# Seven block products for four in the first layer of a mixture-of-experts FFN, with the sums of weights made and kept in the first FFN

## The chip, the cores and the metric

The kernel runs on one core of a Trainium2 chip. The core has a matrix engine (TensorE, in the profile PE, with its weight loads as PEld), a vector engine (VectorE, DVE), an activation engine (ScalarE, ACT), a general engine (GpSimd, POOL) and a queue engine that issues transfers (SyncE, SP). They run side by side and wait for each other by semaphores. The metric is the time of one execution on the device in microseconds (us), the median of several runs.

## The reference

The model is an FFN, an attention-like memory layer and the same FFN again, on 8192 rows of 256 values:

```python
x = L0_attn_hidden
x = x + 0.5 * _L0_ffn_ref(_layernorm(x), gate_w, w1, w2)
x = x + _L0_attn_ref(_layernorm(x), ...)
x = x + 0.5 * _L0_ffn_ref(_layernorm(x), gate_w, w1, w2)
```

Both FFNs use the same weights. An FFN sends every row to the best of E = 8 experts, each with room for CAP = 320 rows:

```python
expert_input = jnp.einsum('tec,td->ecd', sec_mask, tokens)
h = jax.nn.relu(jnp.einsum('ecd,edf->ecf', expert_input, w1))
expert_output = jnp.einsum('ecf,efd->ecd', h, w2)
out = jnp.einsum('tec,ecd->td', combine_weights, expert_output)
```

So the first layer of an expert is a product of 320x256 with 256x1024, and the second layer one of 320x1024 with 1024x256, all in float32.

## The kernel before

`macaron` (from L1309 on) runs the first router, the first FFN (`experts(..., "f1")`), the memory layer (`attention`) and the second FFN (`experts(..., "f2", idle=4)`) one after the other. The router of the second FFN is computed inside the attention.

`experts` goes through the experts e = 0 to 7. Inside it, the instructions of PE, DVE, ACT and POOL stand in the order in which the Python code issues them; each engine works through its own queue in that order. Transfers issued by SP are placed by the compiler. For one expert:

- `gather(e)` (L287) fetches the expert's rows `xg` by three indirect DMAs of POOL, `gate_of(e)` (L298) their gate values by three more. `xg` has four buffers.
- `center` (L311 to L313) takes the mean off each row, on DVE: `bn_stats`, `bn_aggr` and a subtraction for each of three groups of 128 rows (the last has 64). `turn` (L323, L327) transposes the rows on PE into PSUM tiles `pt`, and ACT copies them to `xT`, two chunks of 128 features by 320 rows.
- The first layer, `hidden` (L388, L395): for each of FC = 8 blocks f of 128 hidden values, two matmuls with a 128x128 block of `w1t` as the stationary operand and the 320 columns of `xT` as the moving one, accumulated in a PSUM tile `ph`; ACT applies Relu and writes `hT`. For expert 0 this is done in two passes, over the first 128 rows and then over the other 192, because its rows arrive late.
- The second layer: first the last 64 rows (L419, `py`, both halves of the output in different column groups), then twice 128 rows (L443), with `hT` as the stationary operand. DVE multiplies by the gate and adds the row itself (L429 `xh`, L450 `xo`), and POOL scatters the result by indirect DMAs (L432, L453).

PSUM has eight banks of 512 columns. Before, the tiles of tag `t` (transposes) have three of them, tag `h` (`ph`) three and tag `y` (`py`, and others) two.

Where the rows of an expert lie is found by `Slots`. `begin(q)` counts for the pair of experts 2q and 2q+1: two matmuls into `d_ps`, a copy to `dg` by ACT, one matmul into `b_ps` (L209), a comparison `began` on DVE (L212). `counts(q)` (L228) makes two PSUM tiles `r_ps`, one for each expert of the pair, and `tokens(e)` (L246 to L254) turns one of them into row indices by six short DVE instructions. These searches are put between the blocks of the first layers of experts 0, 1 and 2, by the table `searches`. `keep` issues matmuls whose results nobody reads.

`Weights.load(e)` issues the DMAs of `w1[e]` and `w2[e]`, 1 MB each, from SP; two buffers each. The DMAs for expert e+1 are issued at the start of expert e.

## Time and profile before

| | us |
|---|---|
| median of three runs | 813.77 |
| lowest and highest run | 808.3 and 816.86 |
| the profiled execution | 822.0 |
| its span, from the first instruction to the last | 820.2 |

In the profiled execution the first FFN's experts run from about 51 to 217 us, the attention follows, and the second FFN's experts run from 654 to 820. The granted clock of TensorE was 0.951 of full speed on average. A profile of this kind names a group of instructions by its line in the kernel, its engine, its operation and its tiles (output <- inputs) and gives busy time, mean duration of one and what ended the idle time before. Durations of matmuls overlap, since they are pipelined, so that what one costs is read from start to start.

### The profile page before, as it was taken

The page shows a single profiled execution, that of the slowest core. Times are in us where ns is not written, and L with a number is a line of the kernel's source. Part 1 is how long each engine was busy: PE and PEld are TensorE (multiplying, and loading weights), DVE is VectorE, ACT ScalarE, POOL GpSimd, SP SyncE. Part 2 cuts the span into 40 slices and gives each one's busy share as a digit, 9 for nine tenths or more (in the row PEclk, how much of TensorE's full clock was granted, in tenths as well). Part 3 has the DMA queues.
Part 4 walks back from the last instruction along what each step waited for, and adds up shares of the span by engine and source line. Part 5 has one row for each costly group of instructions (what it writes and reads, how often), then busy time and mean ns, then how long its engine had stood idle before and what let it go on. Part 6 is the DMA issues. An engine that isn't in the chain of part 4 may idle for free. (4 is left out here: it accounts for less than half of the span.)

```text
span 820.2 us, 13993 instructions
## 1 busy us (share of the span) xinstructions
PE 746.9 (91%) x5368; PEld 549.3 (67%) x5368; DVE 452.2 (55%) x941; ACT 348.3 (42%) x756; POOL 472.2 (58%) x606
## 2 busy tenths in 40 slices
PE   7988899999658999899999989999878789999997
PEld 5666678777525485766668576776765466788775
DVE  7772242220228978889886878868743623422220
ACT  5421122222047576757665766756432222122221
POOL 6555244441134778888887889876854344444411
PEclk9998899999968999999997999889988999999999
DMA  9994444451224243443543442434415723454420
GB/s 298 370 382 149 136 138 140 146 166 43 73 66 86 80 104 95 117 152 79 181 105 129 136 121 83 88 119 106 129 60 187 256 72 106 136 175 138 145 68 22
DMA packets 110946, 110.41 MB, mean 135 GB/s; under 512 B 12384, under 2 KB 103904, under 8 KB 110880
## 3 DMA queue, kind: packets, MB, share of 16 engines
q1 hardware_dynamic: 73152, 66.43, 27.2%
q10 hardware_dynamic: 31840, 31.53, 12.2%
q0 software_dynamic: 5888, 11.57, 4.2%
q8 instruction: 42, 0.69, 0.3%
q14 instruction: 24, 0.20, 0.1%
HBM read 78.80 MB, written 30.64 MB: 133 GB/s over the span
## 5 line engine op out<-in xcount | busy, mean ns | idle before, releaser
L395 ACT ACTIVATE hT<-ph 128x320 f32<-128x320 f32 (+2 forms) x144 | 58.4, 408 | 228.8 <-PE ph L388 202.5
L388 PE MATMUL ph<-xT,w1t 128*128 128x320 f32 (+2 forms) x576 | 146.9, 410 | 1.5 <-ACT xT L336 1.5
L388 PEld LDWEIGHTS ph<-xT,w1t 128*128 128x128 f32 x576 | 103.5, 192 | 36.9 <-ACT xT L336 2.3
L443 PE MATMUL py<-w2t,hT 128*128 128x256 f32 x512 | 121.6, 394 | 5.8 <-issue 4.3
L443 PEld LDWEIGHTS py<-w2t,hT 128*128 128x128 f32 x512 | 98.7, 196 | 25.0 <-issue 9.2
L429 DVE SCALAR_TENSOR_TENSOR xh<-py,gate,xg 64x128 f32<-64x128 f32 x32 | 11.2, 350 | 125.2 <-PE py L419 104.2
L450 DVE SCALAR_TENSOR_TENSOR xo<-py,gate,xg 128x256 f32<-128x256 f32 x32 | 15.5, 484 | 93.3 <-PE py L443 93.3
L1144 PE MATMUL pre<-wg,xT 128*128 128x256 f32 x256 | 62.0, 403 | 2.7 <-DVE m L903 2.7
L808 PE MATMUL pre<-xT,w 128*64 128x512 f32 x256 | 61.4, 603 | 0.8 <-ACT kk L840 0.8
L1144 PEld LDWEIGHTS pre<-wg,xT 128*128 128x128 f32 x256 | 51.1, 203 | 11.7 <-DVE m L903 3.3
L298 POOL DMA_INDIRECT gate<-gate_d,get x48 | 45.3, 943 | 21.4 <-issue 13.1
L1188 POOL TENSOR_TENSOR xo<-xo,xr 128x512 f32<-128x512 f32 x32 | 42.9, 1353 | 19.8 <-DVE xo L1182 17.5
L710 ACT ACTIVATE xt<-xt,ln_nm,lx_t 128x256 f32<-128x256 f32 x64 | 34.4, 592 | 24.2 <-POOL ln_nm L705 24.2
L1182 DVE SCALAR_TENSOR_TENSOR xo<-tail,rs,gate 128x256 f32<-128x256 f32 x64 | 27.1, 476 | 26.2 <-DMA out<-xo 12.6
L997 DVE TENSOR_TENSOR gc<-ehd,c 128x1536 f32<-128x1536 f32 x16 | 40.0, 2540 | 0.3
L453 POOL DMA_INDIRECT out<-xo,put x16 | 15.8, 989 | 40.1 <-DVE xo L450 26.7
L453 POOL DMA_INDIRECT x<-xo,put x16 | 15.8, 988 | 38.9 <-DVE xo L450 34.6
L808 PEld LDWEIGHTS pre<-xT,w 128*64 128x64 f32 x256 | 15.8, 136 | 30.3 <-issue 22.3
L432 POOL DMA_INDIRECT x<-xh,put x8 | 8.1, 1006 | 47.7 <-DVE xh L429 47.7
L909 POOL TENSOR_TENSOR abq<-qq,ab 128x512 f32<-128x512 f32 x16 | 33.6, 2105 | 0.9 <-DMA ab<-kept 0.9
L717 PE MATMUL pre<-ident,xt 128*128 128x128 f32 x128 | 21.1, 299 | 14.3 <-ACT xt L710 12.9
L287 POOL DMA_INDIRECT xg<-x,get x24 | 23.4, 974 | 17.6 <-issue 6.1
(259 smaller groups left out, 1622.4 us busy)
## 6 DMA issues: line engine op xcount, KB each, us to landing
w1t<-w_in SPq DMA_DIRECT2D x16, 1024.0 KB
w2t<-w_in SPq DMA_DIRECT2D x16, 1024.0 KB
xt<-hidden_in SPq DMA_DIRECT2D x16, 512.0 KB
x<-xt SPq DMA_DIRECT2D x16, 512.0 KB
xt<-x ACTq DMA_DIRECT2D x16, 512.0 KB
xr<-x ACTq DMA_DIRECT2D x16, 512.0 KB
x<-xo ACTq DMA_DIRECT2D x14, 512.0 KB
out<-xo ACTq DMA_DIRECT2D x14, 512.0 KB
```

The source lines that it names most:

```text
L298: nc.gpsimd.indirect_dma_start(out=gate[:, s : s + 1], out_offset=None, in_=slots.gate, in_offset=bass.IndirectOffsetOnAxis(ap=slots.get[: ...
L388: nc.tensor.matmul(ph[:, at_slots], lhsT=a[:, c, f * P : (f + 1) * P], rhs=at[:, c, at_slots], start=(c == 0), stop=(c == 1),)
L395: nc.scalar.activation(hT[:, f, at_slots], ph[:, at_slots], AF.Relu)
L443: nc.tensor.matmul(py[:, :H], lhsT=hT[:, f, s * P : (s + 1) * P], rhs=b[:, f, :], start=(f == 0), stop=(f == FC - 1),)
L453: nc.gpsimd.indirect_dma_start(out=dst, out_offset=bass.IndirectOffsetOnAxis(ap=slots.put[:, e, s : s + 1], axis=0), in_=xo[:, s, :], in_o ...
L710: self.nc.scalar.activation(x, x, AF.Identity, bias=u.nm[:, j : j + 1], scale=u.r16[:, j : j + 1])
L808: self.nc.tensor.matmul(ps[self.half[r], :], lhsT=self.w3[:, k, f * D : (f + 1) * D], rhs=u.xT[:, k].rearrange("h (p r t) -> h p r t", p=N ...
L909: self.nc.gpsimd.tensor_tensor(u.abq[:, n], u.kv[2], u.ab[:, n], ALU.mult)
L997: self.nc.vector.tensor_tensor(u.gc[:, layer], g.unsqueeze(2).to_broadcast([P, B, 3, D]), u.c3.rearrange("s n j -> s j n").unsqueeze(3).to ...
L1144: self.nc.tensor.matmul(ps[:, q * H : (q + 1) * H], lhsT=u.xT[:, k, j * P : (j + 1) * P], rhs=self.wg[:, k, :], start=(k == 0), stop=(k == 1),
L1182: self.nc.vector.scalar_tensor_tensor(u.xo[h][:, j, :], self.out_of(u, h, j), u.rs[h][:, j : j + 1], u.gate[n][:, j % 2, :], ALU.mult, ALU ...
L1188: self.nc.gpsimd.tensor_tensor(u.xo[h][:, two], u.xo[h][:, two], u.xr[h][:, two], ALU.add)
```

## The change

Both the row halves of `xT` (2 x 160 columns), the two chunks of features and each pair of f blocks are taken as a 2x2 block problem. The plain way has eight block products of 160 columns, done as four matmuls of 320. The changed second FFN does seven block products of 160 columns for each of the four pairs g from expert 1 on (class `First`); expert 0 and the whole first FFN keep the plain way (`plain`). The seven products need four sums of blocks of w1 (`Weights.sums`, 128x512 each) and four sums of blocks of `xT` (`row_sums`, DVE). The results are combined in `hT` by ACT and DVE, in five steps `one` to `five`, of which `four` and `five` of a pair are issued within the next pair; Relu comes last, partly in place.

The sums of weights are made in the first FFN, by GpSimd, at the start of each expert from 1 on, into the four buffers that held the router's rows (tag `xt`), and stored to DRAM (`keep`, 1 MB an expert). The second FFN loads them (1 MB more an expert, two buffers).

With it go these edits: the PSUM banks become two each of tags `x`, `z` (the first layer), `t` (transposes and searches) and `y`; `center` subtracts on ACT, with the sign turned (mean minus row), so that every Relu has a scale of -1; `center(e+2)` is issued after `xh` of expert e, `center(1)` inside expert 0; `gather(e+3)` is issued after the scatter of `xh`, `gate_of(e+1)` at the start of expert e; `begin` is split into `begin` and `began_at`; the searches for later pairs move from the first layers of experts 1 and 2 to the second layers of experts 1, 2 and 3; the part of the second layer on 64 rows takes block f = 6 last; two instructions instead of three prepare `wg` in the attention.

```diff
--- before
+++ after
-    def begin(self, q, between=lambda n: None):
-        nc, sh, pool, pp = self.sh.nc, self.sh, self.pool, self.pp
-        d_ps = pp.tile([P, 512], F32, tag="y", name="d_ps", bufs=2)
+    def begin(self, q, tag="t"):
+        nc, sh = self.sh.nc, self.sh
+        d_ps = self.bank(tag, "d_ps")
         two = slice(q * P, (q + 1) * P)
         nc.tensor.matmul(d_ps[:, :P], lhsT=self.mask[:, two], rhs=sh.tri, start=True, stop=False)
         nc.tensor.matmul(d_ps[:, :P], lhsT=self.prev[:, two], rhs=sh.ntri, start=False, stop=True)
         dg = self.dg[:, q, :]
         nc.scalar.copy(dg[:, :P], d_ps[:, :P])
-        between(1)
-        b_ps = pp.tile([P, 512], F32, tag="h", name="b_ps")
-        nc.tensor.matmul(b_ps[:, 0:1], lhsT=sh.before, rhs=dg[:, P - 1 : P], start=True, stop=True)
-        between(1)
-        began = pool.tile([P, NS * P], F32, tag="began", name="began", bufs=2)
-        nc.vector.tensor_scalar(began, sh.jrow, b_ps[:, 0:1], None, ALU.is_ge)
-        self.began = began
-    def counts(self, q, tag="y"):
+        self.last = dg[:, P - 1 : P]
+    def began_at(self, tag="t"):
+        nc, sh = self.sh.nc, self.sh
+        b_ps = self.bank(tag, "b_ps")
+        nc.tensor.matmul(b_ps[:, 0:1], lhsT=sh.before, rhs=self.last, start=True, stop=True)
+        self.began = self.pool.tile([P, NS * P], F32, tag="began", name="began", bufs=2)
+        nc.vector.tensor_scalar(self.began, sh.jrow, b_ps[:, 0:1], None, ALU.is_ge)
+    def counts(self, q):
...
-            self.pp.tile([P, 512], F32, tag=tag, name="r_ps", bufs={"y": 2, "h": 3}[tag])[
-                :, : NS * (P + 1)
-            ].rearrange("p (s r) -> p s r", s=NS)
+            self.bank("t", "r_ps")[:, : NS * (P + 1)].rearrange("p (s r) -> p s r", s=NS)
...
+    def first(self, e):
         a = self.pool.tile([P, 2, F], F32, tag="w1", name="w1t")
         self.nc.sync.dma_start(a, self.w1[e].rearrange("(c p) f -> p c f", p=P))
-        b = self.pool.tile([P, FC, H], F32, tag="w2", name="w2t")
+        self.w[e] = a
+        v = a.rearrange("p c (g i m) -> p c g i m", i=2, m=P)
+        self.a[e] = [[v[:, c, :, i, :] for c in range(2)] for i in range(2)]
+    def second(self, e):
+        b = self.b[e] = self.pool.tile([P, FC, H], F32, tag="w2", name="w2t")
         self.nc.sync.dma_start(b, self.w2[e].rearrange("(c p) d -> p c d", p=P))
-        self.at[e] = a, b
-def experts(sh, routed, src, dst, weights, dr, name, idle=0):
+    def sums(self, e):
+        s = self.s[e] = self.place().rearrange("p a b -> p (a b)")[:, : 2 * F].rearrange(
+            "p (n g m) -> p n g m", n=4, m=P
+        )
+        if e in self.kept:
+            self.nc.sync.dma_start(s, self.kept[e])
+            return
+        (a11, a12), (a21, a22) = self.a[e]
+        for n, (x, y, op) in enumerate(
+            (
+                (a21, a22, ALU.add),
+                (s[:, 0], a11, ALU.subtract),
+                (a11, a21, ALU.subtract),
+                (a12, s[:, 1], ALU.subtract),
+            )
+        ):
+            self.nc.gpsimd.tensor_tensor(s[:, n], x, y, op)
+    def keep(self, e):
+        self.kept[e] = self.dr.tile([P, 4, FC // 2, P], F32, name=f"sums{e}")
+        self.nc.sync.dma_start(self.kept[e], self.s[e])
+def experts(sh, routed, src, dst, weights, dr, name, idle=0, seven=False):
...
-        pp = st.enter_context(tc.tile_pool(name=f"{name}_p", bufs=3, space=PSUM))
-        slots = Slots(sh, rp, pp, dr, routed)
+        pp = st.enter_context(tc.tile_pool(name=f"{name}_p", bufs=2, space=PSUM))
+        bank = lambda tag, name: pp.tile([P, 512], F32, tag=tag, name=name)
+        slots = Slots(sh, rp, bank, dr, routed)
...
-            ln = ep.tile([P, NS, 8], F32, tag="ln", name="ln")
             xn = ep.tile([P, NS, H], F32, tag="xn", name="xn")
             for s in range(NS):
-                nc.vector.bn_stats(ln[:, s, :6], xg[:, s, :])
-                nc.vector.bn_aggr(ln[:, s, 6:], ln[:, s, :6])
-                nc.vector.tensor_scalar(xn[:, s, :], xg[:, s, :], ln[:, s, 6:7], None, ALU.subtract)
+                ln = ep.tile([P, 8], F32, tag="ln", name="ln", bufs=4)
+                nc.vector.bn_stats(ln[:, :6], xg[:, s, :])
+                nc.vector.bn_aggr(ln[:, 6:], ln[:, :6])
+                nc.scalar.activation(xn[:, s, :], xg[:, s, :], AF.Identity, bias=ln[:, 6:7], scale=-1.0)
...
+        def turn(xn, xT):
+            pts = [bank("t", "pt") for _ in range(2)]
...
+        def row_sums(xT):
+            t = ep.tile([P, 4, HC], F32, tag="xs", name="xs", bufs=1)
+            v = xT.rearrange("p c (j n) -> p (c j) n", j=2)
+            nc.vector.tensor_tensor(t[:, 0:2], v[:, 1:4:2], v[:, 0:2], ALU.subtract)
+            nc.vector.tensor_tensor(t[:, 2], v[:, 3], t[:, 0], ALU.subtract)
+            nc.vector.tensor_tensor(t[:, 3], v[:, 2], t[:, 2], ALU.subtract)
+            return t
...
                 hidden(f, slice(P if e == 0 else 0, CAP))
-                for search, n in searches.get((e, f), ()):
-                    search(n)
                 if (e, f) == (0, 1):
+                    slots.counts(1)
+                    slots.tokens(2)
                     rows.append(gather(2))
-                    gates += [gate_of(1), gate_of(2)]
+                    gates.append(gate_of(1))
+                    xns[1] = center(rows[1])
+                if (e, f) == (0, 3):
+                    slots.tokens(3)
+                if (e, f) == (0, 5):
+                    slots.begin(2)
+                if (e, f) == (0, 6):
+                    slots.began_at()
+            return hT
...
+        class First:
+            def __init__(self, e, xT, t):
+                self.a, self.s = weights.a[e], weights.s[e]
+                self.b = xT.rearrange("p c (j n) -> p c j n", j=2)
+                self.t = t
+                self.hT = ep.tile([P, FC, CAP], F32, tag="hT", name="hT")
+                self.x, self.z, self.u, self.v = {}, {}, {}, {}
+            def product(self, out, a, g, b, start=True, stop=True):
+                nc.tensor.matmul(
+                    out, lhsT=a[:, g, :], rhs=b, start=start, stop=stop, skip_group_check=True
+                )
+            def one(self, g):
+                x = self.x[g] = bank("x", "x")
+                self.product(x[:, :HC], self.s[:, 1], g, self.t[:, 2])
+                self.product(x[:, HC : 2 * HC], self.a[0][0], g, self.b[:, 0, 0], stop=False)
+                p6 = ep.tile([P, HC], F32, tag="p6", name="p6")
+                nc.scalar.copy(p6, x[:, :HC])
+                u = self.u[g] = ep.tile([P, HC], F32, tag="u", name="u", bufs=3)
+                nc.vector.tensor_tensor(u, x[:, HC : 2 * HC], p6, ALU.add)
+            def two(self, g):
+                z = self.z[g] = bank("z", "z")
+                self.product(z[:, :HC], self.s[:, 2], g, self.t[:, 1])
+                self.product(z[:, HC : 2 * HC], self.a[1][1], g, self.t[:, 3])
+                self.product(z[:, 2 * HC : 3 * HC], self.s[:, 0], g, self.t[:, 0], stop=False)
+                v = self.v[g] = ep.tile([P, 1, HC], F32, tag="v", name="v")
+                nc.vector.tensor_tensor(v[:, 0], z[:, :HC], self.u[g], ALU.add)
+            def three(self, g):
+                nc.vector.tensor_tensor(
+                    self.hT[:, 2 * g + 1, :].rearrange("p (j n) -> p j n", j=2),
+                    self.z[g][:, HC : 3 * HC].rearrange("p (j n) -> p j n", j=2),
+                    self.v[g].to_broadcast([P, 2, HC]),
+                    ALU.add,
+                )
+            def four(self, g):
+                x = self.x[g]
+                self.product(x[:, HC : 2 * HC], self.a[0][1], g, self.b[:, 1, 0], start=False)
+                nc.scalar.activation(self.hT[:, 2 * g, :HC], x[:, HC : 2 * HC], AF.Relu, scale=-1.0)
+            def five(self, g):
+                z = self.z[g]
+                self.product(z[:, 2 * HC : 3 * HC], self.s[:, 3], g, self.b[:, 1, 1], start=False)
+                nc.vector.tensor_tensor(self.hT[:, 2 * g, HC:], z[:, 2 * HC : 3 * HC], self.u[g], ALU.add)
+            def relu(self, f, a=0):
+                h = self.hT[:, f, a:]
+                nc.scalar.activation(h, h, AF.Relu, scale=-1.0)
...
+        if seven:
+            weights.sums(1)
...
+        searches = {
+            (1, 0): lambda: slots.counts(2),
+            (1, 1): lambda: slots.tokens(4),
+            (1, 2): lambda: slots.tokens(5),
+            (2, 0): lambda: slots.begin(3),
+            (2, 2): slots.began_at,
+            (3, 0): lambda: slots.counts(3),
+            (3, 1): lambda: slots.tokens(6),
+            (3, 2): lambda: slots.tokens(7),
+        }
+        search = lambda *at: searches.get(at, lambda: None)()
+        for e in range(E):
+            xg, b = rows[e], weights.b[e]
+            if 0 < e < E - 1:
+                if seven:
+                    weights.sums(e + 1)
+                weights.first(e + 1)
+                weights.second(e + 1)
+            if e + 1 < E and e > 0:
+                gates.append(gate_of(e + 1))
+            if e > 0 and not seven:
+                weights.sums(e)
+                weights.keep(e)
+            if not seven or e == 0:
+                hT = plain(e, xn, xT)
+            else:
+                first = First(e, xT, t)
+                hT = first.hT
+                for g in range(G):
+                    first.one(g)
+                    if g > 0:
+                        first.four(g - 1)
+                    first.two(g)
+                    if g > 0:
+                        first.five(g - 1)
+                    first.three(g)
+                    if g > 0:
+                        first.relu(2 * g - 1)
+                        first.relu(2 * g - 2, HC)
+                first.four(G - 1)
+                first.relu(2 * G - 1)
             if e + 1 < E:
-                xT = turn(xn)
+                xT = ep.tile([P, 2, CAP], F32, tag="xT", name="xT")
+                turn(xn[e + 1], xT)
+            if seven and e > 0:
+                first.five(G - 1)
+                first.relu(2 * G - 2, HC)
+            if seven and e + 1 < E:
+                t = row_sums(xT)
             gate = gates[e]
...
+            order = [f for f in range(FC) if f != FC - 2] + [FC - 2]
+            for f in order:
...
+            search(e, 0)
...
+            if e + 2 < E:
+                xn[e + 2] = center(rows[e + 2])
+            search(e, 1)
...
+            if e + 3 < E:
+                rows.append(gather(e + 3))
...
+                if s == 0:
+                    search(e, 2)
...
+        for x, by, op in ((bg, 256.0, ALU.add), (ng, 1.0 / 16.0, ALU.mult)):
+            nc.vector.scalar_tensor_tensor(
+                self.wg, self.wg, by, x.to_broadcast([P, 2, H]), ALU.mult, op
+            )
...
+        place = lambda: rp.tile([P, NI // 4, H], F32, tag="xt", name="s", bufs=4)
...
+        experts(sh, sh.second, x2, out, weights, dr, "f2", idle=4, seven=True)
```

## The prediction

> **What bounds the kernel now.** The page comes first, for the shares of the engines.
>
> ```profile
> span 820.2 us, 13993 instructions
> ...
> PE 746.9 (91%) x5368; PEld 549.3 (67%) x5368; DVE 452.2 (55%) x941; ACT 348.3 (42%) x756; POOL 472.2 (58%) x606
> ```
>
> TensorE (PE) works for nine tenths of the span, but a share over the span says nothing of one stage. So next the table by stretches, for the second FFN (640 to 820 us).
>
> ```profile
> 720.00:740.00 20.00, 20.00 (x111) 16.03 (x110) 4.77 (x14) 4.35 (x10) 9.48 (x10) 1.00 0.45 142
> 740.00:760.00 20.00, 20.00 (x111) 15.98 (x111) 4.29 (x13) 4.35 (x10) 9.00 (x10) 1.00 0.44 148
> 760.00:780.00 20.00, 20.00 (x110) 15.69 (x109) 5.62 (x18) 4.68 (x11) 9.05 (x10) 1.00 0.47 145
> ```
>
> The columns are PE, PEld, DVE, ACT, POOL, the granted clock, the DMA share and GB/s. PE is never idle here, at clock 1.00; DVE is busy 28% at most, ACT 23%, DMA under half. In this stage a nanosecond off PE is a nanosecond off the end, as long as the others can follow. What one expert costs PE is read from the PE timeline: start, duration, group, number of records. A float32 matmul of the program stands as two records, so the 16 matmuls of a first layer are 32.
>
> ```profile
> 753.06 7.17 PE L443 MATMUL py<-w2t,hT 128*128 128x256 f32 x32
> 760.07 8.78 PE L388 MATMUL ph<-xT,w1t 128*128 128x320 f32 x32
> 768.69 0.86 PE L323 MATMUL pt<-ident,xn 128*128 128x128 f32 x6
> 769.48 1.97 PE L419 MATMUL py<-w2t,hT 128*64 128x128 f32 x32
> ```
>
> From start to start: first layer 768.69 - 760.07 = 8.62 us (269 ns a record), transposes 0.79, the 64-row part of the second layer about 1.9, the rest 7.01 (219 ns a record of 256 columns): 18.3 us an expert.
>
> **The seven products on PE.** Per pair of f blocks four matmuls of 320 columns (8 records) become seven of 160 (14 records). No record of 160 columns with its own weight load is in the trace, but expert 0 has its neighbours.
>
> ```profile
> 654.05 1.60 PE L388 MATMUL ph<-xT,w1t 128*128 128x128 f32 x12 [0.46 <-ACT xT L336]
> 655.49 0.38 PE L335 MATMUL pt<-ident,xn 128*128 128x128 f32 x2
> ...
> 661.49 2.87 PE L388 MATMUL ph<-xT,w1t 128*128 128x192 f32 x16
> 664.20 0.38 PE L203 MATMUL d_ps<-tri,mask_b 128*128 128x128 f32 x2
> ...
> 665.16 0.38 PE L209 MATMUL b_ps<-dg,before 128*128 128x1 f32 x2 [0.35 <-ACT dg L206]
> ...
> 666.79 0.86 PE L323 MATMUL pt<-ident,xn 128*128 128x128 f32 x6
> ```
>
> 128 columns: 1.44/12 = 120 ns. 192: 2.71/16 = 169 ns. With 219 at 256 and 269 at 320 these lie on one line, so 160 columns are halfway between the first two: 144.7 ns. One expert: 56 x 144.7 = 8.10 us for 8.62, a gain of 0.52, and 3.6 us over experts 1 to 7. Here a rule of the Trainium skill ("TensorE: Matmul & The Clock Gate", Back-to-back issue gap) would promise more: the warm gap is the columns over 2.4 GHz plus 2.5 ns. The 320-column record fits it with two passes (640/2.4 + 2.7), and 160 would then take 135.8 ns: 7.60 us an expert, 7.1 us in all. The same section warns that the isolated gap undercounts a narrow matmul with a weight load in front. The rows side with the warning: at 128 columns the rule gives 109, the trace 120. I take the rows; 7.1 is the far end of the gain, and 160 columns as dear per column as 128 (150 ns, gain 1.5 us) the near end.
>
> **Who must follow PE.** In before ACT does one Relu of 320 columns per f. Now each pair needs four instructions of ACT and four of DVE in its 14 x 144.7 = 2.03 us. Rows of like shape:
>
> ```profile
> L246 DVE TENSOR_TENSOR upto<-r_ps,jcol 128x384 f32<-128x384 f32 x14 | 7.7, 550 | 5.9 <-PE r_ps L228 5.9
> L246 DVE TENSOR_TENSOR upto<-r_ps,jcol 128x128 f32<-128x128 f32 x2 | 0.6, 290 | 2.4 <-PE r_ps L228 2.4
> ...
> L395 ACT ACTIVATE hT<-ph 128x320 f32<-128x320 f32 x112 | 48.8, 437 | 214.2 <-PE ph L388 190.2 <-issue 15.4 <-PE pt L323 4.5
> L395 ACT ACTIVATE hT<-ph 128x192 f32<-128x192 f32 x16 | 5.2, 330 | 9.6 <-PE ph L388 7.8 <-PE b_ps L209 1.2 <-issue 0.5
> ```
>
> DVE at 160 columns 0.32 us, at 320 0.48: 3 x 0.32 + 0.48 = 1.44. ACT: 3 x 0.31 + 0.44 = 1.4. Both fit into 2.03, with some 0.1 for gaps. The order of waits matters more. A z bank comes back when `five` of two pairs earlier has been added by DVE; followed through (PE result, p6 copy, u, v, five, three) that is about 0.3 us before `two` wants it. I charge nothing inside a stage. After the last pair `five` waits for `three` on DVE: the transposes between cover all but 0.1 us in experts 1 to 6; expert 7 has none, so about 0.9 there. Together 1.5 us. The row sums (three short DVE instructions) are due 7 us later and cost nothing; centering goes from DVE to ACT, which is idle in the second layer.
>
> **Expert 0, in both FFNs.** PSUM banks of tag t fall from three to two, and they now serve the counts, `begin`, `began_at` and the transposes; row statistics of expert 1 move into DVE's queue between `tokens(2)` and `tokens(3)`.
>
> ```profile
> 661.59 0.56 DVE L246 TENSOR_TENSOR upto<-r_ps,jcol 128x384 f32<-128x384 f32 x1 [4.91 <-PE r_ps L228]
> ...
> 663.52 0.55 DVE L246 TENSOR_TENSOR upto<-r_ps,jcol 128x384 f32<-128x384 f32 x1
> ...
> 665.58 0.42 DVE L212 TENSOR_SCALAR began<-jrow,b_ps 128x384 f32<-128x384 f32 x1
> ```
>
> Statistics and mean of three rows take 3 x 0.67 = 2.0 us (0.42 + 0.18 + gaps). `tokens(3)` then starts at 665.5 for 663.5, lets its bank go at 666.9, and `began` behind it ends at about 667.9. The second bank for the transposes is free only then: they start at 667.9 for 666.79, and the second layer queued behind them is late by the same. Its cover, DVE's idleness before the counts, is given up. 1.2 us, in two FFNs 2.4; if the compiler finds another free bank, 0. The first transposes also wait for ACT to center three rows instead of DVE: 0.1 each. The last `begin` and its b_ps leave expert 1's first layer for expert 2's second, where dg is long there, so the 0.35 wait of PE for it goes, twice: -0.7.
>
> **GpSimd in the first FFN.** Its stage holds nine indirect DMAs at 1.25 us from start to start, 11.3 of 18.3 us. Four sums of 128x512 come on top: near row `xo<-xo,xr`, 1353 ns, so 5.6 us with gaps; dear row `abq`, 2105 ns, so 8.6. The sum is 16.9 to 19.9 us: it just fits, or falls back 1.6 us a stage. Behind the sums wait the scatter of xh (ready at 12 us, sums done at 11 to 14) and the gather of expert e+3; this gather is used a stage later, and from expert 5 on there are none. I take 0; with that cover gone it would be up to 6 us. The stores of 1 MB (7 of them) queue on SP ahead of the next weights, which cannot start before their buffer is free at 8.6 us and are due 25 us later: 0. The same for 1 MB more loaded per expert in the second FFN: 8 us of DMA at some 370 GB/s in 18. The first weights already start at 638.5, and the extra load is queued after all of them. The two-for-three wg instructions stand in the idle start of the attention: 0.
>
> **Sum:** -3.6 + 1.5 + 2.4 + 0.2 - 0.7 = -0.2 us. The profiled execution took 822.0 us (820.2 and 1.8 around), 8.2 above the median of 813.77; its sum is 821.8, and I carry the difference over to the median: **813.6 us**. What tells a change of this kernel from none is about 1%, 8.1 us.
>
> **Rivals.** *An old stall goes (faster).* In the second layer of expert 0 PE stands still in this execution, in both FFNs.
>
> ```profile
> 673.39 0.94 POOL L298 DMA_INDIRECT gate<-gate_d,get  x1 [0.30 <-issue]
> ...
> 676.38 0.71 DVE L429 SCALAR_TENSOR_TENSOR xh<-py,gate,xg 64x128 f32<-64x128 f32 x2 [10.37 <-PE py L443]
> ```
>
> xh starts 2.05 us after the last of six gate gathers, though its product ended at 669.6; in the first FFN the gap is the same. PE lost 5.9 and 6.7 us there. Expert 0 now has three of these gathers, ending 3.75 us earlier. If the stall follows them, 7.5 us go, and with the b_ps wait in expert 1 (3.95 and 1.35 us in this execution) 4 to 5 more: about -12, **802 us**. Against it: experts 3 to 6 have the same gathers and no stall at all, and the timed runs lie below the profiled one, so part of this may not be in them.
>
> *The tight chain stalls PE (slower).* In expert 2 of the second FFN two Relus whose products ended at 712.83 and 713.90 came at 715.08 and 715.41, about 2 us late. Three ph banks hid that. With 0.3 us of slack such a delay stops PE, and DVE now waits for PE and ACT four times a pair. 2 us in each of seven stages is 14 us, **827 us**. It decides from 0.3 us per pair on, that is, when DVE's four instructions need over 2.3 us instead of 1.5; 28 pairs at 0.43 cost 12 us. Against it: the like rows above, and clean stages 3 to 6.
>
> *GpSimd binds the first FFN:* +6, 820 us. *The rule's price holds:* -3.5, 810 us. Both are inside 1%, as is my forecast.
>
> **Chances.** Forecast with these two 0.53; stall gone 0.19; tight chain 0.28. The forecast's own range is 808 to 820. To leave out no more than 2 in 10 I reach from 803 to 828.
>
> **What would show it.** Records of 160 columns 145 ns apart at full clock (136 would be the rule); first layers of 8.1 to 8.3 us in experts 1 to 7; transposes of expert 0 about 1 us later, waiting for DVE; no b_ps wait in expert 1; sums of 1.3 to 2.1 us on GpSimd, with no PE wait behind them. PE waiting for DVE v or five inside a stage would prove the slower rival; xh of expert 0 near 672 us the faster.

## The result and the profile after

The kernel after took 822.15 us (median; 817.48 to 829.45) beside 811.14 for the kernel before on the same chip: 1.0114 of it, 95% interval 1.0065 to 1.0163. It is slower; my forecast was no change at 813.6, with slower given 0.28. Of the experiments, half_sums, free_scatters, dve_best and before_again ran on a third chip and the other eight on a second. On both the kernel before takes 797 us; the kernel after takes 820.8 on the second, 1.0275 of it (1.0227 to 1.0323), and was not run on the third. How before differs from chip to chip is told with the run before_again.

The page of the kernel after, its span, the busy times and PE's and POOL's rows of slices (one slice is 20.4 us):

```profile
span 815.7 us, 14687 instructions
...
PE 731.2 (90%) x5536; PEld 555.9 (68%) x5536; DVE 483.7 (59%) x1025; ACT 378.7 (46%) x860; POOL 509.2 (62%) x634
...
PE   7978999999318989999998999999878979999996
...
POOL 6545666654521879888889888876873444444431
```

PE is busy 15.7 us less than in before. But in slices 11 and 12 it falls to 3 and 1: that is the passage from the first FFN to the attention. PE's timeline there, last the idle time before a row and what ended it, first in before and then in after:

```profile
217.40 1.56 PE L598 MATMUL pre<-w,ones 128*128 128x384 f32 x4 [0.58 <-DVE xo L450]
218.79 1.03 PE L598 MATMUL pre<-wg,ones 128*128 128x256 f32 x4
232.75 2.80 PE L717 MATMUL pre<-ident,xt 128*128 128x128 f32 x8 [12.93 <-ACT xt L710]
```

```profile
208.71 1.56 PE L759 MATMUL pre<-w,ones 128*128 128x384 f32 x4 [0.58 <-DVE xo L609]
210.11 1.03 PE L759 MATMUL pre<-wg,ones 128*128 128x256 f32 x4
241.62 2.81 PE L877 MATMUL pre<-ident,xt 128*128 128x128 f32 x8 [30.48 <-ACT xt L870]
```

PE is through with the first FFN 8.7 us earlier than in that profile of before, and begins the attention 8.9 us later: 30.48 us idle for 12.93. ACT is not the cause; it waits for rows of x1 that are not loaded yet. The load (`xt<-x`, issued from ACT's DMA queue) goes out 3.15 us after the last scatter of `xo` in before (at 217.62) and 3.12 after it in after (at 226.48), first before and then after:

```profile
220.77 1.51 ACTq L692 DMA_DIRECT2D xt<-x  x3
...
229.60 1.63 ACTq L852 DMA_DIRECT2D xt<-x  x3
```

The scatters are POOL's. Its timeline for the last expert, in after:

```profile
212.05 1.32 POOL L614 DMA_INDIRECT x<-xo,put  x1 [2.19 <-DVE wg L761]
213.38 1.28 POOL L293 TENSOR_TENSOR s<-w1t 128x512 f32<-128x512 f32 x1
214.74 1.26 POOL L293 TENSOR_TENSOR s<-s,w1t 128x512 f32<-128x512 f32 x1
215.96 1.26 POOL L293 TENSOR_TENSOR s<-w1t 128x512 f32<-128x512 f32 x1
217.18 1.26 POOL L293 TENSOR_TENSOR s<-w1t,s 128x512 f32<-128x512 f32 x1
218.59 0.99 POOL L588 DMA_INDIRECT x<-xh,put  x1 [0.15 <-issue]
223.32 0.97 POOL L614 DMA_INDIRECT x<-xo,put  x1 [3.73 <-DMA x<-xh,put]
226.48 0.97 POOL L614 DMA_INDIRECT x<-xo,put  x1 [2.19 <-issue]
```

PE ended the last `py` at 208.1, and DVE the last `xo` at 208.7. POOL scatters expert 6's `xo` at 212.05, only then makes the sums of expert 7, and scatters expert 7's three parts at 218.59, 223.32 and 226.48. It is a stage behind. The second thing to see is the idle time between two scatters: each waits for a semaphore until the one before has landed in x1 ("<-DMA x<-xh,put").

The second FFN did what the change is for. Some records from its last expert, PE's timeline:

```profile
793.71 0.43 PE L440 MATMUL x<-xs,s 128*128 128x160 f32 x2
...
795.61 0.43 PE L440 MATMUL x<-xs,s 128*128 128x160 f32 x2
...
799.41 0.43 PE L440 MATMUL x<-xT,w1t 128*128 128x160 f32 x2
800.39 0.54 PE L440 MATMUL z<-xT,s 128*128 128x160 f32 x2 [0.54 <-DVE hT L465]
```

From pair to pair 795.61 - 793.71 = 1.90 us for 14 records, 136 ns each, for 2.03 us and 144.7 in my sum.

So three theories stood. **A, GpSimd's backlog**: its stage in the first FFN is longer than PE's, and the attention waits for what is left over. **B, the stores**: 1 MB more an expert holds up the scatters' landings, whoever makes the sums. **C, the second FFN**: the loss lies in the tight chain there, and the passage would be made good elsewhere.

### The profile page after: what moved, and what is told of

It reads as the page before. It is cut to its first block, busy times and chain, and to the rows that moved or that the text cites. A ratio compares the mean times of both kernels' runs of the same rounds, so it can differ in the third digit from the quotient of the medians.

```text
span 815.7 us, 14687 instructions
## 1 busy us (share of the span) xinstructions
PE 731.2 (90%) x5536; PEld 555.9 (68%) x5536; DVE 483.7 (59%) x1025; ACT 378.7 (46%) x860; POOL 509.2 (62%) x634
## 5 line engine op out<-in xcount | busy, mean ns | idle before, releaser
L602 PE MATMUL py<-w2t,hT 128*128 128x256 f32 x512 | 115.3, 382 | 0.3 <-issue 0.3
L602 PEld LDWEIGHTS py<-w2t,hT 128*128 128x128 f32 x512 | 95.7, 190 | 16.3 <-issue 3.4
L394 PE MATMUL ph<-xT,w1t 128*128 128x320 f32 (+2 forms) x352 | 81.9, 387 | 4.4 <-ACT xn L352 2.5
L394 PEld LDWEIGHTS ph<-xT,w1t 128*128 128x128 f32 x352 | 60.2, 190 | 22.8 <-ACT xn L352 2.9
L401 ACT ACTIVATE hT<-ph 128x320 f32<-128x320 f32 (+2 forms) x88 | 33.4, 388 | 78.0 <-PE ph L394 61.2
L1304 PE MATMUL pre<-wg,xT 128*128 128x256 f32 x256 | 59.9, 393 | 3.1 <-DVE m L1063 3.1
L352 ACT ACTIVATE xn<-xg,ln 128x256 f32<-128x256 f32 x48 | 24.3, 508 | 51.8 <-DVE ln L351 37.5
L877 PEld LDWEIGHTS pre<-ident,xt 128*128 128x128 f32 x128 | 15.3, 150 | 36.1 <-ACT xt L870 31.8
```

What stands on the lines that cost most here:

```text
L394: nc.tensor.matmul(ph[:, at_slots], lhsT=weights.w[e][:, c, f * P : (f + 1) * P], rhs=xT[:, c, at_slots], start=(c == 0), stop=(c == 1),)
L401: nc.scalar.activation(hT[:, f, at_slots], ph[:, at_slots], AF.Relu, scale=-1.0)
L602: nc.tensor.matmul(py[:, :H], lhsT=hT[:, f, s * P : (s + 1) * P], rhs=b[:, f, :], start=(f == 0), stop=(f == FC - 1),)
L877: self.nc.tensor.transpose(ps[:, j * P : (j + 1) * P], u.xt[h][:, j, k * P : (k + 1) * P], self.sh.ident)
L1304: self.nc.tensor.matmul(ps[:, q * H : (q + 1) * H], lhsT=u.xT[:, k, j * P : (j + 1) * P], rhs=self.wg[:, k, :], start=(k == 0), stop=(k == 1),
```

## The experiments

All results are ratios to the kernel before on the same chip, with 95% intervals; 0.001 is 0.8 us. "Loss" is the difference from 1. Where a run of the third chip is set beside after_again or dve_both, which ran on the second, the two ratios come from two chips; before takes 797.1 and 797.4 us there.

| run | what it is | ratio | interval |
|---|---|---|---|
| after_again | the kernel after | 1.0275 | 1.0227 to 1.0323 |
| dve_sums | sums on VectorE | 1.0008 | 0.9984 to 1.0031 |
| no_sums | stores, no sums | 1.0007 | 0.9976 to 1.0038 |
| no_store | sums, no stores | 1.0046 | 1.0021 to 1.0072 |
| half_sums | two of four sums on VectorE | 1.0085 | 1.0047 to 1.0123 |
| free_scatters | scatters that don't wait for each other | 0.9999 | 0.9979 to 1.0019 |
| late_sums | sums after the scatters | 1.0217 | 1.0179 to 1.0255 |
| plain_second | second FFN plain | 1.0334 | 1.0281 to 1.0388 |
| dve_early | centering of experts 0, 1 on VectorE | 1.0302 | 1.0255 to 1.0349 |
| dve_both | dve_sums and dve_early | 0.9961 | 0.9932 to 0.9989 |
| dve_best | the same, centering of expert 1 earlier | 0.9902 | 0.9879 to 0.9925 |
| before_again | the kernel before | 1.0000 | 0.9977 to 1.0024 |

### The kernel after on the chip of the others (after_again)

> The kernel after, unchanged, on the chip of the runs it is compared with. It was 1.011 of the kernel before in the first comparison; the kernel without stores 1.0046, the one without sums 1.0007. If the ratio holds on every chip: 1.010 to 1.013.

1.0275: a miss, the loss is more than twice as large there. All further ratios are read against this one. Its timeline of PE shows one more way in which POOL's lateness reaches PE:

```profile
184.05 7.17 PE L602 MATMUL py<-w2t,hT 128*128 128x256 f32 x32
193.66 10.54 PE L394 MATMUL ph<-xT,w1t 128*128 128x320 f32 x32 [2.44 <-DMA w1t<-w_in]
...
244.89 2.80 PE L877 MATMUL pre<-ident,xt 128*128 128x128 f32 x8 [28.68 <-ACT xt L870]
```

Expert 7's first layer waits 2.44 us for its weights and then runs at a lower granted clock (10.54 us for 8.78; 0.66 of full speed from 194 to 199 us). The load of w1 for expert e+2 goes into the buffer that POOL reads for the sums of expert e, and stands on SP behind the store of these sums. POOL late by a stage makes the weights late as well.

### The kernel before once more (before_again)

> The kernel before, unchanged, with a profile on the chip of the other runs, to see whether TensorE's standstill in the second layer of expert 0 and the first layer of expert 1 (some 13 and 9 us in the first and second FFN of the first profile) is there as well. If the kernel before always has it: stages of over 27 us from expert 0 to 1. If it belongs to that profile's chip alone: 19 to 20 us, and the kernel after has nothing to gain from it here. Ratio 1.000.

From the last-64-rows part of expert 0 to that of expert 1 it takes 20.68 us in both FFNs, where the first profile of before had 33.97 and 27.57. So the standstill of 13.3 and 6.9 us belongs to that chip or that run, and not to the kernel. The medians of before are 811 us on that chip and 797 here, 14 us apart, for 20.2 of standstill in the one profile; that it makes the whole difference is likely, but not shown. In the first profile of after the same stages were only 1.6 and 0.7 us longer than in after_again, so that execution of after had little of the standstill. The kernel after took 822.15 us there and 820.76 on the second chip: it is before that differs, and so the change looked better there. What makes it was not tried, and stays open; six gate gathers in a row do not, since before_again has them too and runs through.

### The sums on another engine (dve_sums)

```diff
-            self.nc.gpsimd.tensor_tensor(s[:, n], x, y, op)
+            self.nc.vector.tensor_tensor(s[:, n], x, y, op)
```

> The four sums of weights of the first FFN are made by VectorE and not by GpSimd; nothing else differs from the kernel after. Theory A (GpSimd's backlog: a stage of GpSimd takes 22 to 23 us in the first FFN of the kernel after, for 18.3 to 19.2 on TensorE, so the last scatters land late and the attention's first load with them): GpSimd's queue gets back 5.1 us a stage, the idle time of TensorE ahead of the attention falls from 30.5 us to about 13, and the time by 15 to 18 us, to 804 to 807. Theory B (the 1 MB stores of the sums hold up the scatters' landings, whoever makes the sums): at most half of that comes back, 812 to 818. Theory C (the loss lies in the second FFN, where the tight chain stalls TensorE): no change, 820 to 823.

1.0008 for 1.0275: one word takes the loss away. PE's idle time ahead of the attention is 12.32 us. A sum takes 0.68 us on DVE and 1.27 on POOL. A is borne out, C falls; B too, since the stores are all there.

### Stores without sums, sums without stores (no_sums, no_store)

```diff
# no_sums
-                weights.sums(e)
                 weights.keep(e)
...
-        self.nc.sync.dma_start(self.kept[e], self.s[e])
+        a = self.w[e].rearrange("p a b -> p (a b)").rearrange("p (n g m) -> p n g m", n=4, m=P)
+        self.nc.sync.dma_start(self.kept[e], a)
```

> Leaves out the sums of weights: the first FFN stores the weights themselves in their place (same bytes, same queue), and the second FFN multiplies by these, so its output means nothing; the instructions of the second FFN are the same. Theory A (GpSimd's backlog of 5.1 us a stage): the stores stay and the scatters are on time all the same, 803 to 806, as with the sums on VectorE. Theory B (the stores): as the kernel after or near it, 814 to 822. Theory C (second FFN): 820 to 823.

```diff
# no_store (the second FFN's load, made to fit it, is not shown)
...
-        self.kept[e] = self.dr.tile([P, 4, FC // 2, P], F32, name=f"sums{e}")
-        self.nc.sync.dma_start(self.kept[e], self.s[e])
+        self.kept[e] = self.w1[e].rearrange("(c p) f -> p c f", p=P)
```

> GpSimd makes the sums as in the kernel after, but they are not stored; the second FFN loads the weights themselves in their place (same bytes), so its output means nothing. Theory A (GpSimd's instructions and the waits between its scatters): its stage is three gate gathers 3.9, sums 5.1, scatter to scatter 4.7 and 3.2 and 1.3 for the last, 18.2 us, if the scatters land as fast as those of experts 6 and 7, where nothing else is loaded, and 4 more where the weights' burst of 2 MB goes on beside; I expect part of the backlog to stay, 4 to 10 us of it, so 810 to 817. Theory B (the stores are the cause): all of it goes, 804 to 807. If the stores do nothing at all: 820 to 823.

The absolute times expected came from the first chip; by ratio no_sums gives 1.0007 and no_store 1.0046. The stores alone cost nothing, the sums alone 3.7 us, both together 22. Each of these is measured from before, with the rest of the change in it, since no run leaves out both sums and stores. Together they cost far more than their sum, which neither A nor B had said. What they share is seen in POOL's timeline. No_store, from expert 5's `xh` on:

```profile
175.93 1.01 POOL L589 DMA_INDIRECT x<-xh,put  x1
182.21 1.00 POOL L615 DMA_INDIRECT x<-xo,put  x1 [5.27 <-issue]
...
195.41 1.01 POOL L589 DMA_INDIRECT x<-xh,put  x1
198.47 1.00 POOL L615 DMA_INDIRECT x<-xo,put  x1 [2.05 <-issue]
```

And after_again, the same two experts, with SP's DMA queue below it:

```profile
185.67 1.01 POOL L588 DMA_INDIRECT x<-xh,put  x1
194.43 1.00 POOL L614 DMA_INDIRECT x<-xo,put  x1 [7.76 <-issue]
...
207.65 1.01 POOL L588 DMA_INDIRECT x<-xh,put  x1
212.43 1.00 POOL L614 DMA_INDIRECT x<-xo,put  x1 [3.78 <-issue]
```

```profile
185.54 0.34 SPq L297 DMA_DIRECT2D sums<-s  x1
185.97 0.39 SPq L266 DMA_DIRECT2D w1t<-w_in  x1
186.46 0.89 SPq L274 DMA_DIRECT2D w2t<-w_in  x1
207.52 15.17 SPq L297 DMA_DIRECT2D sums<-s  x2
```

None of these `xo` waits for PE; POOL is behind. From `xh` to `xo` it takes 3.06 us with no other transfer begun beside it (expert 6 of no_store), 4.78 with the 1 MB store (expert 6 of after_again), 6.28 with 2 MB of weights (expert 5 of no_store), and 8.76 with store and weights (expert 5 of after_again): 1.6 to 1.9 us more for each MB. The end of the sums is the moment that releases the store, and with it the weights queued behind, and it is the moment at which POOL goes on to `xh`. In after_again the scatters of `xh` of experts 2 to 5 thus start together with a burst of 3 MB, those of experts 6 and 7 with 1 MB. POOL's stage is 24.2 us from 161.47 to 185.67 in after_again, and 20.3 in no_store (155.66 to 175.93), for 18.3 to 19.2 on PE.

### Half of the sums (half_sums)

```diff
-            self.nc.gpsimd.tensor_tensor(s[:, n], x, y, op)
+            (self.nc.vector if n < 2 else self.nc.gpsimd).tensor_tensor(s[:, n], x, y, op)
```

> The first two of the four sums on VectorE, the last two on GpSimd. A stage of GpSimd was 23 us with four and stays within TensorE's 18.3 to 19.2 with none. If the backlog grows with GpSimd's load: 23 - 2.5 = 20.5 us a stage, 1.5 to 2 over TensorE's, about half of the loss stays: 1.010 to 1.016 of the kernel before. If it was a threshold that half the load stays under: 1.000 to 1.003.

1.0085, the loss is 6.8 us, for 22 in after_again. About a third of it stays, less than the half expected, though the interval reaches into the range expected. PE does not wait for weights in this kernel, and its idle time ahead of the attention is 18.87 us, 5.5 more than in no_sums (13.32). The threshold theory falls.

### Scatters that do not wait (free_scatters)

```diff
-        dst_h = dst.rearrange("n (h d) -> (n h) d", h=2)
+        dst_s = [dst, dst]
+        dst_h = dst
+        if not seven:
+            dst_s[1] = dr.tile([NT, H], F32, name="aside1")
+            dst_h = dr.tile([NT, H], F32, name="aside2")
+        dst_h = dst_h.rearrange("n (h d) -> (n h) d", h=2)
...
-                    out=dst,
+                    out=dst_s[s],
```

> The four sums on GpSimd and the stores as in the kernel after; but in the first FFN each expert's three scatters go to three tensors of the same shape instead of one, so that a scatter does not wait for the one before it to land. Two of the three are never read, so these rows are missing from the attention's input, and the output means nothing; the attention starts after the last scatter to the one tensor that it reads. If the waits between scatters are what makes GpSimd's stage long (4.7 to 8.8 us from xh to xo, 3.2 to 5.3 from xo to xo in the kernel after, for 1.3 without a wait): gates 3.8, sums 5.1, gathers 3.8 and three scatters 3.9 make 16.6 us, under TensorE's stage, and the whole loss goes: 1.000 to 1.005 of the kernel before. If the sums' own time, or the transfers of stores and weights, makes it: 1.015 to 1.027.

0.9999, the whole loss is gone, with four sums on POOL and every store. POOL's timeline for expert 4. POOL is on time here: it waits 0.41 us for DVE's `xh`. In after_again it scatters that `xh` 14 us after PE's part of it:

```profile
146.82 1.01 POOL L593 DMA_INDIRECT aside<-xh,put  x1 [0.41 <-DVE xh L587]
148.14 0.96 POOL L331 DMA_INDIRECT xg<-hidden_in,get  x1 [0.30 <-ACT xn L357]
149.41 0.95 POOL L331 DMA_INDIRECT xg<-hidden_in,get  x1 [0.30 <-issue]
150.66 0.95 POOL L331 DMA_INDIRECT xg<-hidden_in,get  x1 [0.30 <-issue]
151.91 1.01 POOL L619 DMA_INDIRECT x<-xo,put  x1 [0.30 <-issue]
153.69 1.00 POOL L619 DMA_INDIRECT aside<-xo,put  x1 [0.77 <-DVE xo L614]
```

From `xh` to `xo` 5.09 us, all of it the three gathers between and no wait over 0.30 us; no row waits for a landing. That the attention need not wait for two of expert 7's three scatters is not what gains: its first matmul follows 13.28 us of idle time on PE, no less than the 12.32 of dve_sums and the 13.32 of no_sums, where it waits for all three. So it is the wait of one scatter for the landing of the last, made long by transfers beside it, that turns work reckoned at 16.6 us into a stage of 22 to 24. Take away the sums, most of the burst, or the wait, and POOL follows PE.

### The sums after the scatters (late_sums)

```diff
-                weights.sums(e)
-                weights.keep(e)
...
+            if e > 0 and not seven:
+                weights.sums(e)
+                weights.keep(e)
```
(behind an expert's last scatter)

> The same sums on GpSimd and the same stores, but called after an expert's last scatter and not ahead of its first layer. Theory of order (the loss is that the sums and the store's burst stand right ahead of the scatter of xh, and that the last expert's sums are made ahead of the last scatters): the scatters of expert 7 wait for TensorE alone, a store's burst meets gate gathers, and 10 of the 13 us of the last stage's sums and waits go: 0.988 to 0.993 of the kernel after, near 1.000 of before. Theory of load (a stage of GpSimd is 22 to 23 us whatever its order): the backlog stays, the last sums alone leave the end, 5 us: 0.994 of the kernel after, 1.005 of before.

1.0217 of before: both expectations missed that. It is 0.994 of after_again, the number of the theory of load, but by luck, since the trace shows something else. The last scatters do wait for PE alone now (`xo` at 220.22, "<-DVE xo"), as the theory of order said. But PE is late: with the sums of expert e made still later, their buffer and SP's queue give the weights of e+2 later, and PE's stages in the first FFN are 22.8, 19.3, 21.0, 19.5 and 21.8 us from expert 2 on. And the attention still starts late, after 20.43 us of idle time on PE. Its first load goes out 11.1 us after the last scatter, for 3.1 in the kernel after, at the moment at which other work behind the landing of the last sums' store goes on:

```profile
231.31 1.51 ACTq L854 DMA_DIRECT2D xt<-x  x3
...
231.34 0.52 POOL L795 MEMSET st<- 128x512 f32 x1 [4.30 <-DMA sums<-s]
```

So the backlog of the scatters has given way to waits for `w1t` and, it seems, for the last store. Order alone does not cure it.

### The second FFN by itself (plain_second)

```diff
-            if not seven or e == 0:
+            if True:
```
(and no sums loaded, no row sums, no `five` in the second FFN)

> The first FFN as in the kernel after, sums and stores included; the second FFN makes all its first layers by plain products, and loads no sums. This isolates what the seven products give. Theory A: per expert 18.32 - 17.46 = 0.86 us of TensorE's time come back, six in all, less about 1.5 of waits after the last pair and inside the chain: 4 to 5 us slower than the kernel after, 826 to 827. Theory C (the tight chain costs more than the seven products give): faster than the kernel after, 812 to 818.

1.0334 for 1.0275: 4.7 us slower without the seven products. The traces agree: from the start of the 64-row part of expert 0 to the start of the last two 128-row parts, those of expert 7, the second FFN takes 131.81 us plain and 126.77 with seven products, a gain of 5.04.

### The early centering (dve_early, dve_both, dve_best)

Two rows of PE's timeline and one of ACT's, from the kernel after's expert 0 in the first FFN:

```profile
53.78 1.60 PE L394 MATMUL ph<-xT,w1t 128*128 128x128 f32 x12 [1.49 <-ACT xT L383]
...
64.95 0.92 PE L394 MATMUL ph<-xT,w1t 128*128 128x192 f32 x4 [1.24 <-ACT xn L352]
```

```profile
63.09 1.59 ACT L352 ACTIVATE xn<-xg,ln 128x256 f32<-128x256 f32 x3 [3.12 <-DVE ln L351]
```

ACT's copy of the first 128 rows (`xT`) stands in its queue behind the centering of the rows that land later, and three centerings of 0.51 us stand ahead of the Relus that free PE's banks. So:

```diff
# dve_early, and with sums on VectorE dve_both
-                nc.scalar.activation(xn[:, s, :], xg[:, s, :], AF.Identity, bias=ln[:, 6:7], scale=-1.0)
+                if early:
+                    nc.vector.tensor_scalar(xn[:, s, :], xg[:, s, :], ln[:, 6:7], -1.0, ALU.subtract, ALU.mult)
+                else:
+                    nc.scalar.activation(xn[:, s, :], xg[:, s, :], AF.Identity, bias=ln[:, 6:7], scale=-1.0)
...
-                    xns[1] = center(rows[1])
+                    xns[1] = center(rows[1], True)
...
-        xn[0], xT = center(rows[0]), ep.tile([P, 2, CAP], F32, tag="xT", name="xT")
+        xn[0], xT = center(rows[0], True), ep.tile([P, 2, CAP], F32, tag="xT", name="xT")
```

> Rows 0 and 1 of the experts (the ones whose centering stands ahead of or inside the first layer of expert 0) are centered by VectorE in one instruction, as in the kernel before; all else as in the kernel after. Expected: the first layer of expert 0 starts 2.5 us earlier in the first FFN, since ScalarE's copy of xT no longer stands behind three centerings, and 1.24 of wait for hT goes in each FFN: 3 to 5 us faster than the kernel after if GpSimd's backlog does not hide the first FFN's part; if the backlog hides it (the attention waits for the scatters, not for TensorE), only the second FFN's 1 us: 0 to 2 us.

> Both: the sums on VectorE and the early centering on VectorE. With the backlog gone TensorE's start sets the end of the first FFN, so here the early centering is worth its 3 to 5 us: 0.994 to 0.996 of the kernel with the sums on VectorE (1.0008 of before), so 0.994 to 0.997 of before, faster than both kernels.

Alone it gives nothing (1.0302 beside 1.0275; the intervals overlap): the last scatter of the first FFN goes out at 229.52 us, for 230.39 in after_again, so the backlog hides what PE gains there. In the second FFN nothing is gained either: PE's wait of 1.24 us for ACT goes, and waits for DVE of 1.71 and 0.54 us come in its place. With the backlog gone it gives 0.9961 for 1.0008, 3.7 us. The waits for DVE are there too. PE's timeline in dve_both:

```profile
65.49 0.30 PE L364 MATMUL pt<-ident,xn 128*128 128x128 f32 x1 [1.71 <-DVE tok L249]
66.33 0.81 PE L364 MATMUL pt<-ident,xn 128*128 128x128 f32 x5 [0.54 <-DVE began L214]
67.07 1.97 PE L574 MATMUL py<-w2t,hT 128*64 128x128 f32 x32
```

The transposes wait for the banks that `tokens(3)` and `began` read, and these stand in DVE's queue behind expert 1's statistics and centering. The last version moves those to where before had them (shown against dve_both):

```diff
-                    xns[1] = center(rows[1], True)
...
         turn_one(xn[0], xT, 0)
+        xn[1] = center(rows[1], True)
```

> Sums on VectorE, rows 0 and 1 of the experts centered by VectorE, and those of expert 1 ahead of the first layer of expert 0 as in the kernel before (VectorE is idle there), not behind its second search. In the run with both edits the transposes of expert 0 waited 1.71 and 0.54 us for VectorE's tokens and began. If that is the order of VectorE's queue alone, these 2.2 us go in both FFNs: 0.990 to 0.992 of the kernel before (both edits: 0.9961). If another wait takes their place: 0.995 to 0.997.

0.9902 (0.9879 to 0.9925): 7.8 us faster than before, and 4.7 us better than dve_both, for the 4.4 or so expected (2.2 in each FFN). Its rows of PE have neither wait:

```profile
50.68 1.60 PE L397 MATMUL ph<-xT,w1t 128*128 128x128 f32 x12 [0.46 <-ACT xT L386]
...
652.35 0.87 PE L364 MATMUL pt<-ident,xn 128*128 128x128 f32 x6
653.14 1.97 PE L574 MATMUL py<-w2t,hT 128*64 128x128 f32 x32
```

This version beats both kernels: its interval lies wholly below 1.

## Why the prediction was wrong, by its own steps

**GpSimd in the first FFN: the step that failed.** I took 0 for it, out of nine indirect DMAs at 1.25 us and the sums of weights. The sums were sized well (four at 1.27, 5.1 us). The scatters were not: 1.25 us is the pitch of gathers, which do not wait for each other's landing; a scatter to x1 waits for the last one's. Before hides that, since its scatters come in PE's pace, 3.4 us apart in experts 5 to 7. But one place in the trace of before would have shown it, expert 0, where DVE made `xh` late and the first `xo` only 2 us behind it:

```profile
73.33 1.02 POOL L432 DMA_INDIRECT x<-xh,put  x1 [3.12 <-DVE xh L429]
76.39 1.00 POOL L453 DMA_INDIRECT x<-xo,put  x1 [2.04 <-issue]
80.07 0.98 POOL L453 DMA_INDIRECT x<-xo,put  x1 [2.68 <-DVE xo L450]
```

`xh` to `xo` 3.06 us, though POOL had nothing else to do and DVE ended that `xo` at 75.0 us, 1.4 before its scatter: that is the price of a late scatter, and the floor only, with no transfer begun beside it. Expert 4's stage in after_again is, from `xh` to `xo` with the gathers inside it, 8.8 us, from `xo` to `xo` 5.3, the last scatter 1.3, the gates 3.5 and the sums with their gaps 5.2: 24.2 us, for my 16.9 to 19.9. The rest of the step fell with it. "From expert 5 on there are no gathers" is no relief, because in the kernel after the gathers lie inside the wait from `xh` to `xo` (8.83 us with them, 8.76 without, in after_again). And the lag is paid: the five stages from expert 1's `xh` to expert 6's take POOL 22.0 to 24.2 us, for 18.3 to 19.2 on PE, and stand at the end as about a stage of delay.

**The stores at 0** failed with it. I had the next weights wait only until PE was through with their buffer, at 8.6 us of a stage. POOL's sums hold it much longer when POOL is behind: in after_again the first layer of expert 5 ended at 163.2 us and POOL's sums of its weights at 185.5, and so expert 7's weights came 2.44 us late. And the store is released at the very moment at which POOL scatters `xh`, and lengthens the landing. Without the sums the stores cost nothing (no_sums); with them they turn 3.7 us into 22.

**The rival "GpSimd binds the first FFN" (+6)** was the right mechanism with a price for the sums alone. On the second chip it is worth some +22, paid in two places: PE waits for weights (2.44 us in after_again), and the attention starts late.

**The seven products** were undersized. 136 ns a record, not 144.7. The rule of the Trainium skill ("TensorE: Matmul & The Clock Gate", Back-to-back issue gap) that I set aside for the interpolation gave 135.8, with two passes a record, and holds here; 128 and 192 columns in expert 0 lie above it (120 and 169 ns for 109 and 162.5), and it was wrong to draw a line from them to rows from a different sequence. Net gain 5.04 us in the second FFN, for 3.6 - 1.5 = 2.1.

**The chain inside a stage** was right at zero: three waits of 0.65, 0.26 and 0.17 us in the first profile of after, none in after_again. The rival of a tight chain fell. The wait for the last pair's `five` in expert 7 is 0.54 us, for 0.9.

**Expert 0** came out near in size and other in cause. I had 1.2 us for PE's transposes behind DVE; measured is 1.24 of wait for ACT, behind whose centerings the Relus stand. The predicted wait seems to be hidden behind it: in after_again PE's transposes start at 69.05, and `began` ends at 68.91, so that without the 1.24 it would be some 1.1 us (an estimate from these times). Dve_both shows it at 2.25, with expert 1's three subtractions, 0.35 us each or more, on DVE as well. The "0.1 each" for centering on ACT held in the second FFN; in the first the copy of `xT` starts at 53.38 us for 50.34 in before (of which 0.3 to 0.4 was there before it: `gates` starts at 48.59 for 48.18), since the centering of rows that land later stands ahead of it: some 2.6 to 2.7 us.

**The b_ps wait** in expert 1 went, as said. **The old stall** is not in before on the third chip. On the first chip it was mostly gone in the profile of after, as that rival had it, which is the likely reason that the loss was 1.1% there and not 2.7; why it went stays open.

## What to carry to other kernels

An engine with time to spare on average may have none in the stage where work is added; sum its stage with the waits of its own queue, and take their price from a place where that engine was late, not from one where it was kept waiting anyway. Look at what a finished instruction releases: here the end of the sums released up to 3 MB of transfers just when the next scatter had to land. And when an edit brings nothing alone, try it again with the binding cost removed: the early centering gave nothing beside the backlog, 3.7 us without it, and 8.4 once it stood in its right place (dve_best, for dve_sums).

## What the runs showed of the hardware

- In this program an indirect scatter to the same tensor as the last one waits for a semaphore until that has landed: 3.06 us from issue to issue with no other transfer begun beside it, 4.78, 6.28 and 8.76 us with 1, 2 and 3 MB started in the same moment. A gather, or a scatter to another tensor, follows at 1.25 to 1.3 us.
- After a standstill of PE of 2.34 and 2.54 us (half_sums and free_scatters) the mean granted clock between 52 and 56 us was 0.75 and 0.62, and the next 12 records, those of expert 0, took 1.87 and 2.75 us for 1.60. After the wait of 2.44 us for weights in after_again it was 0.66 over 5 us. In dve_best and dve_both, without the standstill, it stays at 1.00 between 52 and 56. A wait of PE there cost more than its length; that the standstill is the cause was not tested by itself.
